# Which tiles of a softmax denominator VectorE sums: nine instead of eight in the second and fourth head pair

## The chip, the cores and the metric

The kernel runs on one core of one Trainium2 chip. The metric is the device time of one launch in microseconds (us). Before the change the median of three runs is 4265.29 us (4264.81 to 4266.23).

## The reference, cut to what matters

Two graph attention layers follow each other, each with a residual and a layer norm, on eight batches of 2048 nodes with 256 features.

```python
# layer 0: eight heads of 32 features
e = leaky_relu(e_src[..., :, None] + e_dst[..., None, :], 0.2)
e = e + (softplus(beta_tilde) * log(prior + 1e-6))[:, None, :, :]     # prior = adj
e = where(adj > 0, e, neg_inf)
h = einsum('bhij,bhjf->bhif', softmax(e, -1), x_proj)
x = layernorm(x + h.transpose(...).reshape(B, N, D) @ W_out.T)
# layer 1: one head
e = where(adj > 0, leaky_relu(einsum('bnd,bmd->bnm', x @ W1, x @ W2), 0.2), -1e12)
x = layernorm(x + relu(softmax(e, -1) @ (x @ W3)))
```

A softmax needs a numerator (the weights times the projected features) and a denominator (the sum of the weights). The change concerns how the denominator of layer 0 is summed, and nothing else.

## The kernel before, in words

**Layer 0, the class `Gat`.** The eight heads are worked in four pairs (`hp` = 0 to 3), and each pair in 16 steps (`jt` = 0 to 15), one for each tile of 128 source nodes j. A step makes one tile `s` of 128 x 2048 float32 for each of the two heads, on VectorE (L391). Its 128 partitions are the nodes j, its 2048 columns the nodes i. The operands are a broadcast row `c` of the head, a per-partition factor `re`, and a tile `mt` of the transposed mask, which a DMA fetches for each step. TensorE then multiplies `s` with the features: `products(self.val, ...)` issues 8 matmuls (the trace shows 16, two for each), which add the numerator up in the PSUM tile `val` over the 16 steps (L424). The denominator is the same product with a weight that does not depend on the feature: `products(self.den, ...)` with `e[:, jt, h]` broadcast to 32 columns, 8 more matmuls into the PSUM tile `den`, also at L424.

**The chain.** A tile j can be taken out of the `den` matmuls and summed elementwise instead. The list `SUMMED[b][hp]`, called `chain` in `step`, holds the tiles of which this is done. In the step of its first tile, ScalarE makes for each head a scaled copy `d = s * e` (L409). For each further tile of the chain, VectorE adds `d = s * e + d` for each head (L404). That update stands one step later in the source: in step `jt` the update is for tile `jt - 1`, behind the two `s` of step `jt`. After step 15 eight matmuls with a weight of ones (L424, `den<-d,ones`) fold the two sums `d` into `den`. A tile in the chain so saves 8 `den` matmuls and costs two passes of VectorE over 128 x 2048 values. The first tile that is not in the chain starts the accumulation in `den`.

**Which tiles.** The first pair has no chain, in any batch. Batch b = 0 has none at all, b = 1 has six tiles in the other three pairs, and b = 2 to 7 have the eight even tiles (0, 2, ... 14) in each of them.

**Layer 1, the class `Dot`.** It takes 128 rows of nodes at a time, 16 row steps for a batch. A row step issues on TensorE four groups of four transposes (`pt`, L590) of the exponentials `p`, between them the scores `e` (L564) of the next row, and then the products with `h3` (`acc`, L607). ScalarE evicts the scores (L566) and the transposes (L592), VectorE applies the mask and finds the row's extreme in one pass over 128 x 2048 values (L569), and ScalarE takes the exponential (L572), which the next row step's transposes wait for.

**How the two are woven.** While batch b - 1 goes through `Dot`, batch b goes through `Gat` (the loop at the end of the kernel). The first pair's steps run beside the output projection and layer norm of layer 0 and the transposes of `turn`. Then `dot.scores(0)` makes the scores of the first row. The first row step takes steps 0 and 1 of the second pair before its transposes and steps 2 and 3 behind its `acc`. Twelve further row steps take 4, 4, 4 (second pair), 3, 3, 3, 3, 4 (third pair) and 3, 3, 3, 3 (fourth pair, whose last 4 are in the thirteenth). Each such group of 3 or 4 steps stands behind the `acc` of its row, so on TensorE all of a group's `val` and `den` matmuls come in one block.

**What sets the order.** TensorE's instructions stand in source order (`tc.manual_schedule`), and from the end of batch 0's layer 0 SyncE's DMA issues too. VectorE's and ScalarE's are placed by the framework when the kernel is built: of what it takes to be ready, it prefers what stands earlier in the source. The trace shows that it moves instructions past each other: of a group's last two `s`, one often stands behind an update of the chain that comes later in the source. [...]

**Buffers.** `s` tiles come from a ring of eight slots, which also holds layer 1's `p` and, for part of a batch, half of `ht`. A slot comes free when its `val` matmuls, its `den` matmuls and, for a chain tile, its update are done. `d` has two slots.

Of the kernel before, what the change touches and what calls it, by code (L numbers as in the profile page):

```python
# [27 lines left out]
def kernel(  # L28
# [27 lines left out]
    B, N, D = x.shape  # L56
    H, _, DH = w_proj.shape
    NT = N // P
# [5 lines left out]
    NP = H // HP  # L64
# [1 line left out]


    SUMMED = [[()] * NP, [()] + [(0, 3, 6, 8, 11, 14)] * (NP - 1)]
    SUMMED += [[()] + [tuple(range(0, NT, 2))] * (NP - 1)] * (B - 2)

    const = ctx.enter_context(tc.tile_pool(name="const", bufs=1))
    dram = ctx.enter_context(tc.tile_pool(name="dram", bufs=1, space=DRAM))
# [695 lines left out]
```

## Time and profile before

| what | value |
|---|---|
| median of the runs | 4265.29 us (4264.81 to 4266.23) |
| the profiled execution: its time, its span | 4269.6 us, 4267.8 us |
| granted TensorE clock | 0.995 |
| TensorE `val` (L424) | 8192 matmuls, 980.3 us busy |
| TensorE `den<-s,re` (L424) | 5600 matmuls, 686.2 us busy |
| VectorE `s` (L391) | 1024 instructions, 2358.4 us busy, 2341 ns each |
| VectorE `d` (L404) | 282 instructions, 654.2 us busy, 2342 ns each |
| ScalarE `d` (L409) | 42 instructions, 84.4 us busy, 2011 ns each |

The busy time of a group is the union of its instructions' spans, and times inside the trace count from the span's start. The `den` matmuls are 350 tiles with 16 matmuls each (512 steps of 8 batches, less 162 tiles in chains). The scaled copies at L409 show how regular the kernel is: those of the second pair start at 1098.24, 1591.89, 2085.83, 2579.86, 3073.66 and 3567.41 us in batches b = 2 to 7. So one of these batches, b = 4, is read closely, and counted six times. There the first `val` matmul of the four pairs starts at 1979.0, 2088.7, 2218.6 and 2345.2 us, and that of the next batch at 2472.6 us.

### The profile page before, as it was taken

What the parts mean: (1) busy time and instruction counts of PE and PEld (TensorE: products, weight loads), DVE (VectorE), ACT (ScalarE), POOL (GpSimd) and SP (SyncE); (2) the same over time, 40 slices, a digit from 0 to 9 for tenths busy, and PEclk for the clock granted to TensorE, in tenths of its full rate; (3) what the DMA queues carried; (4) which work ended last, traced back from release to release, by engine and by line L of the source; (5) the groups of instructions that cost most, each with busy time, mean ns of one, the idle gap of its engine ahead of it and who ended that gap; (6) DMA issues with size and microseconds to landing.
All of it is one profiled execution on the core that took longest, in us unless ns stands there. A gap on an engine that the chain in (4) does not pass through costs nothing.

```text
span 4267.8 us, 59104 instructions
## 1 busy us (share of the span) xinstructions
PE 4169.3 (98%) x24928; PEld 2234.3 (52%) x24928; DVE 3617.9 (85%) x2432; ACT 1606.5 (38%) x3007; POOL 10.3 (0%) x14
## 2 busy tenths in 40 slices
PE   7999999999999999999999999999999999999999
PEld 4444355555555555555555555555455555555766
DVE  6888779998899979999799988999799997998222
ACT  6522133332333333332433333333333323343554
POOL 0000000000000000000000000000000000000000
PEclk9999999999999999999999999999999999999999
DMA  7988756656455565556555474555555565553211
GB/s 240 312 281 322 243 205 225 235 203 238 175 203 201 192 212 181 193 191 226 187 203 194 161 250 166 204 194 204 204 186 189 182 233 180 203 187 136 78 48 40
DMA packets 268458, 843.52 MB, mean 198 GB/s; under 512 B 33184, under 2 KB 166304, under 8 KB 194464
## 3 DMA queue, kind: packets, MB, share of 16 engines
q1 hardware_dynamic: 232352, 806.17, 53.7%
q10 hardware_dynamic: 35840, 33.57, 2.3%
q8 instruction: 195, 3.19, 0.3%
q14 instruction: 71, 0.58, 0.0%
HBM read 763.76 MB, written 75.37 MB: 197 GB/s over the span
## 4 chain that ended last, share of the span: by engine, by line
PE 57%; DVE 26%; issue 8%; DMA 4%; ACT 4%; SPq 0%; DVEq 0%; POOL 0%; ACTq 0%; POOLq 0%
DVE s L391 16%; PE acc L607 13%; PE e L564 12%; PE val L424 12%; PE den L424 8%; DVE d L404 5%; PE pt L590 3%; DMA mt<-mt_d 2%; PE h3p L532 2%; PE proj L283 2%; PE h1p L553 2%; DVE p L569 2%; PE y L493 1%; ACT d L409 1%; DMA adj_r<-in_adj_dram 1%
## 5 line engine op out<-in xcount | busy, mean ns | idle before, releaser
L391 DVE SCALAR_TENSOR_TENSOR s<-c,re,mt 128x2048 f32<-128x2048 f32 x1024 | 2358.4, 2341 | 180.9 <-DMA mt<-mt_d 58.0
L424 PE MATMUL val<-s,v 128*32 128x512 f32 x8192 | 980.3, 598 | 24.1 <-DVE s L391 24.1
L564 PE MATMUL e<-x1t,h 128*128 128x512 f32 x2048 | 964.7, 595 | 6.1 <-ACT pts L592 5.1
L607 PE MATMUL acc<-h,pts 128*128 128x256 f32 x4096 | 907.5, 380 | 0.0
L607 PEld LDWEIGHTS acc<-h,pts 128*128 128x128 f32 x4096 | 779.5, 190 | 157.4 <-issue 57.4
L424 PE MATMUL den<-s,re 128*32 128x512 f32 x5600 | 686.2, 594 | 0.0
L404 DVE SCALAR_TENSOR_TENSOR d<-s,re,d 128x2048 f32<-128x2048 f32 x282 | 654.2, 2342 | 0.0
L424 PEld LDWEIGHTS val<-s,v 128*32 128x32 f32 x8192 | 252.6, 110 | 601.5 <-issue 528.5
L569 DVE CUSTOM_DVE_ANT_0 p<-p,pen 128x2048 f32<-128x2048 f32 x128 | 292.6, 2286 | 256.2 <-ACT p L566 256.1
L564 PEld LDWEIGHTS e<-x1t,h 128*128 128x128 f32 x2048 | 351.2, 190 | 271.7 <-issue 249.8
L566 ACT ACTIVATE p<-e 128x512 f32<-128x512 f32 x512 | 306.1, 598 | 392.9 <-PE e L564 387.5
L572 ACT ACTIVATE p<-p,neg 128x2048 f32<-128x2048 f32 x128 | 256.5, 2004 | 496.8 <-DVE neg L569 496.8
L424 PEld LDWEIGHTS den<-s,re 128*32 128x32 f32 x5600 | 190.3, 110 | 419.4 <-issue 419.0
L590 PEld LDWEIGHTS pt<-ident,p 128*128 128x128 f32 x2048 | 245.5, 141 | 301.1 <-issue 235.8
L592 ACT COPY pts<-pt 128x512 f32<-128x512 f32 x512 | 297.5, 586 | 200.3 <-PE pt L590 193.9
L590 PE MATMUL pt<-ident,p 128*128 128x128 f32 x2048 | 310.2, 276 | 15.7 <-ACT p L572 8.3
L230 ACT ACTIVATE f<-mv,eps_ln 128x1 f32<-128x1 f32 x128 | 37.9, 296 | 432.7 <-DVE mv L228 431.7
L612 ACT ACTIVATE z<-acc,rec 128x256 f32<-128x256 f32 x128 | 60.1, 470 | 288.5 <-issue 127.5
L283 PE MATMUL proj<-wp,xt 128*128 128x272 f32 (+1 forms) x512 | 130.6, 400 | 3.6 <-ACT xt L182 1.8
L532 PE MATMUL h3p<-w3s,x1t 128*128 128x256 f32 x512 | 122.7, 383 | 6.4 <-ACT x1t L527 4.7
L493 PE MATMUL y<-wot,ht 128*128 128x256 f32 x512 | 119.0, 385 | 3.5 <-ACT x1t L527 2.1
L285 ACT COPY v<-proj 128x256 f32<-128x256 f32 x128 | 47.2, 374 | 198.0 <-PE proj L283 153.5
(88 smaller groups left out, 1896.4 us busy)
## 6 DMA issues: line engine op xcount, KB each, us to landing
mt<-mt_d SPq DMA_DIRECT2D x496, 1024.0 KB
c<-c_d SPq DMA_DIRECT2D x64, 1024.0 KB
pen<-pen_d SPq DMA_DIRECT2D x112, 512.0 KB
xg<-in_x_dram SPq DMA_DIRECT2D x60, 512.0 KB
adj_t<-in_adj_dram SPq DMA_DIRECT2D x16, 1024.0 KB
mt_d<-mt SPq DMA_DIRECT2D x16, 1024.0 KB
rb<-rec_d SPq DMA_DIRECT2D x128, 128.0 KB
x_d<-ht ACTq DMA_DIRECT2D x64, 256.0 KB
```

The costliest lines, as they stand in the source:

```text
L283: nc.tensor.matmul(t[:, 0:cols], xt[kc][:, ts(it % IG, P)], wp[:, kc, 0:cols], start=(kc == 0), stop=(kc == KC - 1))
L391: nc.vector.scalar_tensor_tensor(sa, self.cs[a], self.re[:, 0, jt, h:h + 1], mt, ALU.max, ALU.mult)
L404: nc.vector.scalar_tensor_tensor(d, sa, e[:, jt - 1, h:h + 1], d, ALU.mult, ALU.add)
L424: nc.tensor.matmul(dst[ts(q, DH), ts(c, BK)], weights[q % 2], s[q % 2][:, ds(q // 2 * HALF + c * BK, BK)], start=start, stop=stop)
L532: nc.tensor.matmul(t[:, ts(i, D)], x1t[:, kc, ts(2 * (j - lag) + i, P)], w3s[:, kc, :], start=(kc == 0), stop=(kc == KC - 1))
L564: nc.tensor.matmul(t, self.h1[:, kc, ts(it % IG, P)], self.x1t[:, kc, ts(c, BK)], start=(kc == 0), stop=(kc == KC - 1))
L566: nc.scalar.activation(p[:, ts(c, BK)], t, AF.Prelu, alpha=ALPHA)
L569: nc.vector.tensor_tensor_reduce(p, p, pen, -1.0, FMAX, ALU.add, ALU.min, neg)
L572: nc.scalar.activation(p, p, AF.Exp, bias=neg, scale=-1.0, accum_out=den)
L590: nc.tensor.transpose(t[:, ts(k, P)], p[:, ts(g * IG + k, P)], ident)
L592: nc.scalar.copy(pt, t)
L607: nc.tensor.matmul(acc, pts[g][:, ts(k, P)], self.h3[:, j, :], start=(j == 0), stop=(j == NT - 1))
```

## The change

For batches b = 2 to 7, the second pair's chain becomes tiles 0, 1, 2, 3, 6, 8, 10, 12, 14: tiles 1 and 3 come in, tile 4 goes out. The third pair's stays as it was. The fourth pair's becomes 0, 2, 4, 5, 7, 9, 11, 12, 14: tiles 5, 7, 9, 11 come in, 6, 8, 10 go out. Both have nine tiles in place of eight. Batches 0 and 1 are as before. No function changes, only the list that `step` reads.

```diff
     SUMMED = [[()] * NP, [()] + [(0, 3, 6, 8, 11, 14)] * (NP - 1)]
-    SUMMED += [[()] + [tuple(range(0, NT, 2))] * (NP - 1)] * (B - 2)
+    SUMMED += [[(), (0, 1, 2, 3, 6, 8, 10, 12, 14), tuple(range(0, NT, 2)), (0, 2, 4, 5, 7, 9, 11, 12, 14)]] * (B - 2)
```

The lines of `step` that read it:

```python
chain = SUMMED[self.b][hp]
if jt - 1 in chain[1:]:
    for d, sa, h in zip(self.sums, self.last, heads):
        nc.vector.scalar_tensor_tensor(d, sa, e[:, jt - 1, h:h + 1], d, ALU.mult, ALU.add)
...
if jt not in chain:
    self.products(self.den, [e[:, jt, h:h + 1].to_broadcast([P, DH]) for h in heads], s,
                  jt == min(set(range(NT)) - set(chain)), not chain and jt == NT - 1)
```

## The prediction

> **What bounds the kernel now.** I read the page's busy shares first, then one batch (b = 4) by head pair, then the engines' timelines where a wait ends.
>
> ```profile
> PE 4169.3 (98%) x24928; PEld 2234.3 (52%) x24928; DVE 3617.9 (85%) x2432; ACT 1606.5 (38%) x3007; POOL 10.3 (0%) x14
> ```
>
> TensorE (PE) is nearly always busy, and VectorE (DVE) has 15% left. Whether that rest lies where the change puts work is seen from the busy times by stretch (columns: stretch, its length, then busy us and instructions of PE, PEld, DVE, ACT, POOL):
>
> ```profile
> 1979.00:2088.70 109.70, 108.02 (x749) 55.21 (x749) 83.88 (x59) 33.20 (x66) 0.00 (x0) 1.00 0.68 235
> 2088.70:2218.60 129.90, 127.44 (x729) 67.76 (x728) 127.88 (x81) 50.37 (x85) 0.00 (x0) 1.00 0.50 179
> 2218.60:2345.20 126.60, 126.31 (x729) 67.30 (x728) 123.43 (x81) 48.15 (x86) 0.00 (x0) 1.00 0.57 201
> 2345.20:2472.60 127.40, 126.51 (x729) 67.10 (x728) 120.72 (x79) 46.54 (x87) 0.00 (x0) 1.00 0.50 179
> ```
>
> VectorE idles 25.8 us in the first pair, 2.0 in the second, 3.2 in the third, 6.7 in the fourth. So the second pair is bound by both engines at once, and the spare time is mostly in the pair that the change leaves alone. The start of the second pair on VectorE:
>
> ```profile
> 2071.01 4.62 DVE L391 SCALAR_TENSOR_TENSOR s<-c,re,mt 128x2048 f32<-128x2048 f32 x2 [1.04 <-PE den L424]
> 2090.72 2.29 DVE L569 CUSTOM_DVE_ANT_0 p<-p,pen 128x2048 f32<-128x2048 f32 x1 [15.10 <-ACT p L566]
> ...
> 2093.21 9.04 DVE L391 SCALAR_TENSOR_TENSOR s<-c,re,mt 128x2048 f32<-128x2048 f32 x4
> 2102.17 4.61 DVE L404 SCALAR_TENSOR_TENSOR d<-s,re,d 128x2048 f32<-128x2048 f32 x2
> 2106.69 2.28 DVE L569 CUSTOM_DVE_ANT_0 p<-p,pen 128x2048 f32<-128x2048 f32 x1
> ```
>
> Behind the `s` of steps 0 and 1 VectorE stands 15.1 us in front of the mask pass of layer 1's first row, which needs the last score eviction. From 2090.7 on it has no gap until 2323.3. On ScalarE and then TensorE at the same place:
>
> ```profile
> 2085.83 1.99 ACT L409 ACTIVATE d<-s,re 128x2048 f32<-128x2048 f32 x1
> 2087.72 0.59 ACT L566 ACTIVATE p<-e 128x512 f32<-128x512 f32 x1
> 2088.20 2.00 ACT L409 ACTIVATE d<-s,re 128x2048 f32<-128x2048 f32 x1
> 2090.09 0.60 ACT L566 ACTIVATE p<-e 128x512 f32<-128x512 f32 x1
> ```
>
> ```profile
> 2092.12 1.90 PE L424 MATMUL den<-s,re 128*32 128x512 f32 x16
> 2095.20 0.66 PE L590 MATMUL pt<-ident,p 128*128 128x128 f32 x4 [1.18 <-ACT p L572]
> ```
>
> The `d` that an update of tile 1 would continue exists only from 2087.8 (head 0) and 2090.2 (head 1), late in the gap. And TensorE, done with the `den` of tile 1, waits for the exponential. At the end of the second pair (VectorE, then TensorE):
>
> ```profile
> 2186.92 9.13 DVE L391 SCALAR_TENSOR_TENSOR s<-c,re,mt 128x2048 f32<-128x2048 f32 x4
> 2195.97 4.60 DVE L404 SCALAR_TENSOR_TENSOR d<-s,re,d 128x2048 f32<-128x2048 f32 x2
> ```
>
> ```profile
> 2200.62 1.92 PE L424 MATMUL den<-d,ones 128*32 128x512 f32 x14 [0.15 <-DVE d L404]
> ```
>
> The last `s` is ready at 2196.05, and its `val` matmuls start at 2196.02 with the first head: no lead is left. The group before ended with 0.3 us of lead (`s` ready 2164.76, `val` 2165.04), the one before that with 1.9. The end of the fourth pair on VectorE:
>
> ```profile
> 2422.16 9.14 DVE L391 SCALAR_TENSOR_TENSOR s<-c,re,mt 128x2048 f32<-128x2048 f32 x4 [1.98 <-PE den L424]
> ...
> 2442.47 4.61 DVE L404 SCALAR_TENSOR_TENSOR d<-s,re,d 128x2048 f32<-128x2048 f32 x2
> 2447.00 4.61 DVE L391 SCALAR_TENSOR_TENSOR s<-c,re,mt 128x2048 f32<-128x2048 f32 x2
> ```
>
> Here the update of tile 14 was placed ahead of step 15's `s`, which end at 2451.6, and TensorE waits for them (1.8 us between two `val` matmuls).
>
> [...] Here two updates from 2102.17 to the next start at 2106.69 are 2.26 us each, start to start, so listed durations overlap by 0.08; I use 2.26. [...] I therefore price `den` by starts: `val` and `den` alternate at 2067.32, 2069.06, 2070.78 and 2072.49, so 1.72 us each, not the 686.2/350 = 1.96 us of the busy sum.
>
> **The change, part by part.** Per batch it adds two tiles to the chains: VectorE gets 4 updates, 4 x 2.26 = 9.0 us, and TensorE loses 2 x 1.72 = 3.4 us of `den`. Over six batches that is 54 us and 20.6 us. No DMA moves: an update issues none, SyncE's and POOL's queues keep their order, and the copy at L409 stays with tile 0. That `den` in the second pair now starts with tile 4 instead of 1 costs nothing: its eviction was done at 2080. No update carries a wait that is new in kind: it needs an `s` and the `d` before it.
>
> *Second pair, TensorE.* Removing tile 1's `den` (2092.12 to 2093.8) lengthens the wait for the exponential, which still ends at 2095.2: worth nothing. Exchanging tile 3 for tile 4 brings the next row forward by 1.72 us and takes it back in the next group: nothing at tile 7. So TensorE gains 0.
>
> *Second pair, VectorE.* Tile 3's update replaces tile 4's; both stand before step 7's `s`. Tile 1's is 4.52 us more. It is written behind step 2's `s`, and can go forward into the 15.1 us gap only behind its `d`. The framework placed the copies between score evictions, so when step 1's `s` was done it counted the mask pass, which comes first in the source, as ready or nearly. I take it that the update stands behind the mask pass, where nothing idles: +4.52 us for every later `s`. The leads of 1.9, 0.3 and 0.0 turn into TensorE waits that sum to 4.5 us at step 15. The mask pass of the second row may come 4.5 us later too; its exponential then ends near 2115.5, and the transposes, due at 2114.4 without tile 3's `den`, would start before their old 2116.2: no loss. Net **+4.5 us**. Bounds: +1.8 (both updates ahead of the mask pass, 2090.2 + 2.26 against 2090.72), +4.5.
>
> *Third pair.* Both engines come 4.5 us later, so leads stay: 0.
>
> *Fourth pair.* Up to step 11 the updates only change places (leads there 7.8 to 11 us, more than one update). In the last group there are three updates of tiles, 11, 12 and 14, for two before. The extra 4.52 us meets 0.69 + 1.98 = 2.7 us of idle before step 12's `s`. The 1.98 is a wait for a ring slot until tile 9's `den` ended; tile 9 is in the chain now, so the slot is free anyway, and some 0.7 us for the row's residual add stays. I take 2.0 us as absorbed: +2.5 us for step 14's `s`. Step 15's slot comes free 1.72 us sooner and VectorE comes 2.5 later, so step 15's `s` is probably no longer passed by tile 14's update: its `s` ends 2451.6 + 2.5 - 4.5 = 2449.6, and tile 14's update at 2454.1, where the `den<-d,ones` matmuls, due about 2455.1 before, can start. Net **-1.0 us**. If the update stays ahead, step 15's `s` is late by 2.5 us: +2.5. The best is the `den` saved, -1.7.
>
> *Sum.* 6 x (4.5 - 1.0) = +21 us. The profiled execution took 4269.6 us (span 4267.8 and 1.8 around it), 4.3 above the median of the runs, or 0.1%; I put the 21 us on the median: **4286 us**.
>
> **Rivals.**
> *B, both pairs bound by VectorE:* tile 14's update stays ahead. 6 x (4.5 + 2.5) = +42, 4307 us. For it: that is the order now. Against: the shift that I worked out for step 15.
> *C, the update of tile 1 uses the end of the gap:* +1.8 (both heads in it) or +2.26 (one head), with -1.0: 6 x 0.8 to 6 x 1.26, so 4270 to 4273 us; 4291 if the fourth pair goes as in B. For it: updates do pass waiting instructions elsewhere, as at 2442.47.
> *D, faster:* the two copies at L409 move ahead on ScalarE. Their `s` are done at 2065.3 and 2070.0, and ScalarE idles 4.7 us before 2072.7. If the second copy ends by 2086.2, both updates fit in front of 2090.7 for nothing, and the last eviction no longer waits behind a copy: it could run at 2088.8 instead of 2090.09, so the row's exponential and all behind it come 1.3 us sooner. 6 x (-1.3 - 1.0) = -14, 4251 us. Against: what feeds the copies isn't changed by the edit.
> That the edit doesn't do what it says I exclude: `step` reads the list directly.
>
> **How the numbers follow.** Forecast 0.40; B 0.25; C 0.20 (0.07 of it at 4291); D 0.12; worse than 4312 us 0.03. What a measurement of this kernel can tell from no change is about 0.2%, or 8.5 us. Faster: D and a little, 0.13. Same: C at 4270 to 4273, 0.13. Slower: 0.74. The range leaves out D and the worst: 4262 to 4312 us, the lower end being C with the best fourth pair (6 x (1.8 - 1.7), 4266) less 4 us.
>
> **What would show it.** L404 should count 282 + 24 = 306 and `den<-s,re` 5600 - 192 = 5408. Step by step: tile 1's update behind the mask pass at the second pair's start and a wait for the exponential of about 2.9 us instead of 1.18; TensorE's waits for `s` in the second pair summing to some 4.5 us; that pair 134.5 us long instead of 129.9, the third 126.6, the fourth 126.4. I am wrong if the second pair is no longer than before, which would mean updates in the gap, or if the fourth grows, which would mean tile 14's update still ahead of step 15.

## The result and the profile after

The changed kernel takes 4300.3 us (median of 4 runs, 4295.29 to 4304.79), the kernel before 4265.76 us (4 runs, 4264.81 to 4266.41). The ratio is 1.0078, with a 95% interval from 1.0066 to 1.0090: slower by 0.8%, 34.5 us. The forecast was 4286 us.

The busy shares after:

```profile
PE 4166.4 (97%) x24736; PEld 2224.8 (52%) x24736; DVE 3668.9 (85%) x2456; ACT 1606.8 (37%) x3007; POOL 10.7 (0%) x14
```

VectorE's busy time grew by 51 us (24 more updates) and TensorE's shrank by 3 (192 matmuls fewer): L404 counts 306 instructions and `den<-s,re` 5408, as the prediction named them. As a share of the longer span VectorE is where it was and TensorE one point lower. The shares tell nothing of why. The busy times of one batch (b = 4) by head pair do, with the columns as before:

```profile
1987.10:2096.80 109.70, 108.02 (x745) 55.19 (x745) 83.88 (x59) 33.19 (x66) 0.00 (x0) 1.00 0.68 235
2096.80:2231.70 134.90, 127.74 (x713) 66.61 (x712) 132.77 (x83) 50.49 (x85) 0.00 (x0) 1.00 0.49 173
2231.70:2358.90 127.20, 126.44 (x729) 67.32 (x728) 122.70 (x81) 47.76 (x86) 0.00 (x0) 1.00 0.58 198
2358.90:2486.80 127.90, 125.43 (x717) 66.61 (x720) 125.02 (x81) 46.82 (x87) 0.00 (x0) 1.00 0.50 180
```

The second pair went from 129.9 to 134.9 us, with VectorE busy for all but 2.1 us of it, as before. The third grew by 0.6, the fourth by 0.5, though 16 of its matmuls are gone. The start of the second pair, on VectorE:

```profile
2079.54 4.61 DVE L391 SCALAR_TENSOR_TENSOR s<-c,re,mt 128x2048 f32<-128x2048 f32 x2 [0.39 <-DMA mt<-mt_d]
2098.86 2.29 DVE L569 CUSTOM_DVE_ANT_0 p<-p,pen 128x2048 f32<-128x2048 f32 x1 [14.70 <-ACT p L566]
...
2101.34 4.52 DVE L391 SCALAR_TENSOR_TENSOR s<-c,re,mt 128x2048 f32<-128x2048 f32 x2
2105.77 4.61 DVE L404 SCALAR_TENSOR_TENSOR d<-s,re,d 128x2048 f32<-128x2048 f32 x2
2110.30 4.61 DVE L391 SCALAR_TENSOR_TENSOR s<-c,re,mt 128x2048 f32<-128x2048 f32 x2
```

The pair of updates at 2105.77 is tile 1's. It stands behind the mask pass and step 2's `s`; the long gap is as empty as before, and step 3's `s` is pushed back by it. TensorE in the same place, and at the ends of the groups of steps 4 to 7, 8 to 11 and 12 to 15:

```profile
2103.34 0.66 PE L590 MATMUL pt<-ident,p 128*128 128x128 f32 x4 [2.90 <-ACT p L572]
...
2149.59 1.49 PE L424 MATMUL val<-s,v 128*32 128x512 f32 x11 [1.22 <-DVE s L391]
...
2177.47 1.49 PE L424 MATMUL val<-s,v 128*32 128x512 f32 x11 [0.73 <-DVE s L391]
...
2208.76 1.49 PE L424 MATMUL val<-s,v 128*32 128x512 f32 x11 [0.65 <-DVE s L391]
...
2213.28 1.92 PE L424 MATMUL den<-d,ones 128*32 128x512 f32 x14 [0.89 <-DVE d L404]
```

The wait for the exponential is 2.90 us instead of 1.18: it grew by just the 1.72 us of tile 1's `den`. Then each group ends in a wait for an `s` or a `d`, where before there was 0.15 us in all. In these lines the waits for an `s` or a `d` sum to 3.5 us, less than the 4.5 us that the prediction named as a sign; how late the pair's last block is in the end is worked out further below.

Over batches 2 to 7 the pairs' lengths, from the first `val` matmul of a pair to that of the next, sum as follows in the profiled executions (us). For the last pair of batch 7 the length goes to the end of its last `val` matmul. Tables below use the same sums.

| kernel | first pair | second | third | fourth |
|---|---|---|---|---|
| before | 664.8 | 779.9 | 759.5 | 745.7 |
| after | 660.7 | 809.9 | 763.2 | 746.4 |

The difference is 30.3 us (-4.1, +30.0, +3.7, +0.7), and the two profiled executions, 4269.6 and 4300.06 us, are 30.5 apart. The first pair's -4.1 us lies almost wholly in batch 2 (115.8 against 111.6 us) and is not the change's doing: executions with the old first pair show 660 as well as 665. In those with 665, the kernel before among them, the granted clock of TensorE is 0.50 for 6.8 us near the start of that pair (there from 1003.0 us on); in the changed kernel's it isn't.

### The profile page after: what moved, and what is told of

The parts are those of the page before. It is cut to its first block, busy times and chain, and to the rows that moved or that the text cites. A ratio compares the mean times of both kernels' runs of the same rounds, so it can differ in the third digit from the quotient of the medians.

```text
span 4298.3 us, 58706 instructions
## 1 busy us (share of the span) xinstructions
PE 4166.4 (97%) x24736; PEld 2224.8 (52%) x24736; DVE 3668.9 (85%) x2456; ACT 1606.8 (37%) x3007; POOL 10.7 (0%) x14
## 4 chain that ended last, share of the span: by engine, by line
PE 49%; DVE 32%; issue 10%; DMA 5%; ACT 3%; SPq 0%; DVEq 0%; ACTq 0%; POOL 0%; POOLq 0%
DVE s L391 19%; PE acc L607 11%; PE e L564 10%; PE val L424 9%; DVE d L404 8%; PE den L424 8%; PE pt L590 3%; DMA mt<-mt_d 3%; DVE p L569 2%; PE h3p L532 2%; PE proj L283 2%; PE h1p L553 2%; PE y L493 1%; ACT d L409 1%; DMA c<-c_d 1%
## 5 line engine op out<-in xcount | busy, mean ns | idle before, releaser
L424 PE MATMUL val<-s,v 128*32 128x512 f32 x8192 | 1001.2, 599 | 37.1 <-DVE s L391 37.0
L564 PE MATMUL e<-x1t,h 128*128 128x512 f32 x2048 | 968.9, 597 | 13.0 <-ACT pts L592 12.5
L404 DVE SCALAR_TENSOR_TENSOR d<-s,re,d 128x2048 f32<-128x2048 f32 x306 | 712.1, 2343 | 0.0
L424 PE MATMUL den<-s,re 128*32 128x512 f32 x5408 | 676.9, 594 | 0.0
L439 ACT COPY ht<-val 64x1024 f32<-64x1024 f32 x64 | 64.5, 1008 | 202.0 <-PE val L424 198.7
```

Of the source, the lines that this page charges most:

```text
L404: nc.vector.scalar_tensor_tensor(d, sa, e[:, jt - 1, h:h + 1], d, ALU.mult, ALU.add)
L424: nc.tensor.matmul(dst[ts(q, DH), ts(c, BK)], weights[q % 2], s[q % 2][:, ds(q // 2 * HALF + c * BK, BK)], start=start, stop=stop)
L564: nc.tensor.matmul(t, self.h1[:, kc, ts(it % IG, P)], self.x1t[:, kc, ts(c, BK)], start=(kc == 0), stop=(kc == KC - 1))
```

## The experiments

The theory after the result: tile 1's update in the second pair is the whole loss, because VectorE has no gap from the first row's mask pass on, and TensorE gains nothing by tile 1. Its rivals: each ninth tile costs alike; or the crowding of tiles 1, 2, 3 costs. Every ratio is to the kernel before, in runs on the same chip.

**Second pair only.**

```diff
+[(), (0, 1, 2, 3, 6, 8, 10, 12, 14), tuple(range(0, NT, 2)), tuple(range(0, NT, 2))]
```

> Second pair as changed, fourth pair with its old eight even tiles. Theory (the ninth tile's update of the second pair lands in a stretch in which VectorE has no gap, and TensorE gains nothing there): 5.0 us for the second pair and 0.6 for the third behind it, six times: +30 to +34 us, nearly the whole loss. Rival (each of the two ninth tiles costs its two VectorE passes wherever it stands): half of the loss, +15 to +19 us.

Measured: 4302.54 us against 4264.27, ratio 1.0094 (1.0080 to 1.0108). The second pair alone makes the whole loss. At 38 us it is above the 30 to 34 expected, and 4 above both pairs together, though the intervals overlap. The table behind the run with tile 1 alone shows where that comes from.

**Fourth pair only.**

```diff
+[(), tuple(range(0, NT, 2)), tuple(range(0, NT, 2)), (0, 2, 4, 5, 7, 9, 11, 12, 14)]
```

> Fourth pair as changed, second pair with its old eight even tiles. Theory: the ninth tile finds VectorE idle there (6.7 us of 127.4) and TensorE saves 1.7 us less what the last group waits, so -1 to +0.5 us a batch: -6 to +3 us. Rival (each ninth tile costs alike): +15 to +19 us.

Measured: 4264.56 us, ratio 1.0002 (0.9993 to 1.0010). With the second pair as it was, the ninth tile is free in the fourth and worth nothing either. That each ninth tile costs alike is refuted.

**Tile 3 for tile 4.**

```diff
+[(), (0, 2, 3, 6, 8, 10, 12, 14), tuple(range(0, NT, 2)), tuple(range(0, NT, 2))]
```

> Second pair with eight tiles, 0, 2, 3, 6, 8, 10, 12, 14: tile 3 in for tile 4, tile 1 not in the chain. Theory (only tile 1 costs): within 3 us of before. Rival (the chain's tiles standing close together early in the pair hold back the tiles s behind them): +10 us or more.

Measured: 4263.08 us, ratio 0.9999 (0.9991 to 1.0007). The exchange costs nothing.

**Tile 1 alone.**

```diff
+[(), (0, 1, 2, 4, 6, 8, 10, 12, 14), tuple(range(0, NT, 2)), tuple(range(0, NT, 2))]
```

> Second pair with nine tiles, 0, 1, 2, 4, 6, 8, 10, 12, 14: tile 1 in, tile 4 stays, tile 3 is not in the chain. Theory: the same loss as with the second pair changed as a whole, +27 to +34 us. Rival (the crowding of tiles 1, 2, 3 is what costs): +15 us or less.

Measured: 4301.55 us, ratio 1.0088 (1.0074 to 1.0102), as with the whole second pair. The crowding is refuted; it is tile 1. The pairs' lengths in these runs:

| kernel | first pair | second | third | fourth |
|---|---|---|---|---|
| second pair only | 660.4 | 810.1 | 763.2 | 751.3 |
| fourth pair only | 662.3 | 779.9 | 761.5 | 744.7 |
| tile 1 alone | 659.7 | 810.5 | 763.2 | 752.0 |

Both runs with tile 1 in the second pair came out above what was expected of them. Their fourth pair, whose chain is the old one, is about 6 us longer than before (745.7), and longer than the changed kernel's (746.4). The expectations had counted the second pair and the third alone.

The next two take the two sides of tile 1 apart.

**Tile 1's matmuls taken away, without the update.**

```diff
-if jt - 1 in chain[1:]:
+if jt - 1 in chain[1:] and not (self.b > 1 and hp == 1 and jt == 2):
```

> Second pair as with tile 1 alone added (0, 1, 2, 4, 6, ... 14), but tile 1's update is left out too, so its share is missing from that pair's denominators: TensorE is rid of 8 matmuls a batch (1.72 us) and VectorE gets nothing for it. Theory (behind tile 1's matmuls TensorE waits for the exponential anyway): no gain, within 3 us of before. Rival (TensorE is the bound, every block of matmuls taken away is worth its length): -10 us.

Measured: 4271.81 us against 4267.02, ratio 1.0011 (1.0004 to 1.0017). Nothing is gained, and 4.8 us are even lost, a little more than the 3 us expected at most. Where the time went, on TensorE:

```profile
2093.42 1.90 PE L424 MATMUL val<-s,v 128*32 128x512 f32 x16
2098.21 0.66 PE L590 MATMUL pt<-ident,p 128*128 128x128 f32 x4 [2.90 <-ACT p L572]
2098.71 3.09 PE L564 MATMUL e<-x1t,h 128*128 128x512 f32 x4
```

The `den` that is gone became wait, 2.90 us. Then four score matmuls take 3.09 us instead of 1.88: the granted clock (the share of TensorE's full clock, third figure from the end) falls.

```profile
2098.00:2100.00 2.00, 1.79 (x7) 1.04 (x8) 2.00 (x2) 0.75 (x3) 0.00 (x0) 0.81 0.46 170
2100.00:2102.00 2.00, 2.00 (x5) 0.86 (x4) 2.00 (x2) 0.11 (x1) 0.00 (x0) 0.50 0.19 25
2102.00:2104.00 2.00, 2.00 (x8) 1.26 (x7) 2.00 (x2) 1.07 (x2) 0.00 (x0) 0.84 0.86 332
```

This happens in four of the six batches, whose second pair is 131.0 us long. In the other two it is 130.0 us, as before: the matmuls are worth nothing without the fall, too.

**Tile 1's matmuls kept, and the update as well.**

```diff
-if jt not in chain:
+if jt not in chain or self.b > 1 and hp == 1 and jt == 1:
```

(The accumulation in `den` then starts with tile 1.)

> As with tile 1 alone added, but its denominator matmuls are kept as well, so that tile counts twice in that pair's denominators: VectorE gets the update and TensorE is rid of nothing. Theory (the loss is VectorE's alone and the matmuls taken away were worth nothing): the same as tile 1 alone, +33 to +40 us. Rival (the matmuls taken away gave 10 us back, the update cost 47): +44 us or more.

Measured: 4306.23 us against 4267.02, ratio 1.0093 (1.0079 to 1.0107), the same as tile 1 alone within the intervals. With the `den` back, the wait in front of the transposes is the old one:

```profile
2108.78 1.90 PE L424 MATMUL den<-s,re 128*32 128x512 f32 x16
2111.86 0.66 PE L590 MATMUL pt<-ident,p 128*128 128x128 f32 x4 [1.18 <-ACT p L572]
```

So the loss is VectorE's update alone, and the matmuls that it replaces were worth nothing. It isn't the clock either, which could have been the cause as it also falls behind the 2.90 us wait of the changed kernel: in this run it falls in no second pair of batches 2 to 7, and each of them is 134.9 us long, as there.

**The update moved into the gap.** A new function makes `s` of steps 0 and 1, the copies of tile 0 and, where tile 1 is in the chain, its update ahead of the first row's scores. TensorE's order is unchanged. Chains as in the run with the second pair only. (Shown is the call of the new function.)

```diff
+if fresh and b > 1:
+    fresh.early()
 dot.scores(0)
```

> Second pair as changed, fourth as before; in batches 2 to 7 the tiles s of steps 0 and 1, the two scaled copies of tile 0 and tile 1's update stand in the source ahead of the first row's scores, so they are placed ahead of its score evictions and its mask pass. Theory (the update costs because it cannot use the 15 us in which VectorE waits for the last score eviction, as its copy is late): the update lies in that gap, and the last eviction no longer waits behind a copy: -1.3 to +0.5 us a batch, so -10 to +3 us. Rival (nine tiles are one too many for the second pair wherever the update stands): +20 us or more.

Measured: 4269.85 us, ratio 1.0006 (0.9998 to 1.0014): 35 us better than the same chains without it (2.8 us above the kernel before, instead of 38.3). ScalarE makes the copies 20 us sooner, and VectorE puts tile 1's update (here L446) where it had waited:

```profile
2062.75 2.00 ACT L444 ACTIVATE d<-s,re 128x2048 f32<-128x2048 f32 x1 [1.41 <-DVE s L435]
...
2066.74 2.00 ACT L444 ACTIVATE d<-s,re 128x2048 f32<-128x2048 f32 x1 [0.54 <-DVE s L435]
```

```profile
2072.56 4.61 DVE L446 SCALAR_TENSOR_TENSOR d<-s,re,d 128x2048 f32<-128x2048 f32 x2
...
2079.78 6.78 DVE L396 SCALAR_TENSOR_TENSOR s<-c,re,mt 128x2048 f32<-128x2048 f32 x3
...
2086.63 2.29 DVE L597 CUSTOM_DVE_ANT_0 p<-p,pen 128x2048 f32<-128x2048 f32 x1
```

That is the mechanism of rival D of the prediction, and the update is free by it. But the gain that D promised behind it didn't come. The run moves the copies and the update together, so it doesn't show which of the two had kept the update out of the gap. A late copy isn't all of it: in the changed kernel head 0's copy ended at 2095.96, 2.9 us before the mask pass, and VectorE, idle for those 2.9 us, still took its update of 2.26 us behind that pass, in the order placed.

**The same with eight tiles.** To see what the early copies do by themselves: chains as before the change, with the same function.

> The old eight tiles everywhere, with the tiles s of steps 0 and 1 of the second pair and the two scaled copies placed early, as in the run with the copies early and nine tiles. Theory (early copies free the last score eviction, 1.2 us a batch, and that is all they do by themselves): -7 us, and the nine tiles bring nothing on top, so the same as that run within 5 us once its longer third pair is left out. Rival (the ninth tile, once its update is free, gives TensorE's 1.72 us): 10 us slower than the run with nine tiles.

Measured: 4267.08 us against 4267.03, ratio 1.0000 (0.9991 to 1.0008). The ninth tile is worth nothing even when it is free, and the 7 us expected of the early copies didn't come. They do shorten the second pair, and the third gives it back:

| kernel | first pair | second | third | fourth |
|---|---|---|---|---|
| before | 664.8 | 779.9 | 759.5 | 745.7 |
| early, nine tiles | 662.5 | 772.8 | 769.0 | 745.4 |
| early, eight tiles | 661.4 | 770.9 | 772.3 | 745.4 |

With eight tiles TensorE no longer waits at the first transposes of the second pair of batch 4 (with nine it waits 1.58 us there). In the third it waits for ScalarE, twice in this batch:

```profile
2223.42 1.98 PE L592 MATMUL e<-x1t,h 128*128 128x512 f32 x4 [1.47 <-ACT pts L620]
...
2273.63 1.98 PE L592 MATMUL e<-x1t,h 128*128 128x512 f32 x4 [1.41 <-ACT h L583]
```

ScalarE, at the second of them, had the row's norm in front of the eviction, and the norm waited 7.4 us for VectorE:

```profile
2271.03 0.30 ACT L230 ACTIVATE f<-mv,eps_ln 128x1 f32<-128x1 f32 x1 [7.41 <-DVE mv L228]
...
2272.99 1.07 ACT L583 COPY h<-h1p 128x512 f32<-128x512 f32 x2 [0.47 <-ACT z L234]
```

What TensorE wins in the second pair it loses in the third, where ScalarE's queue stands behind VectorE.

**A chain in the first pair.** VectorE's spare time lies there.

```diff
+[(10, 12, 14), tuple(range(0, NT, 2)), tuple(range(0, NT, 2)), tuple(range(0, NT, 2))]
```

> Second to fourth pair as before; the first pair gets a chain of its own in batches 2 to 7, tiles 10, 12, 14: two updates for each head (9.0 us of VectorE), and on TensorE three blocks of denominator matmuls less and one block with ones more (3.4 us less). Theory (spare VectorE time is in the first pair, whose tiles s are 8 us or more ahead there, and TensorE sets its length): -3.4 us a batch, -15 to -20 us. Rival (an update costs what VectorE takes for it, wherever it is put): slower, +20 us or more.

Measured: 4254.54 us against 4267.02, ratio 0.9966 (0.9954 to 0.9979), faster than both kernels. The first pair of the batch read here:

```profile
1977.20:2084.10 106.90, 104.47 (x716) 54.13 (x715) 92.58 (x63) 37.17 (x68) 0.00 (x0) 1.00 0.68 240
```

It is 106.9 us long instead of 109.7: 2.8 of the 3.4 us of matmuls saved are gained, and VectorE has 14 us left over there. The 12.5 us are less than the 15 to 20 expected.

**Four tiles in the first pair.**

```diff
+[(10, 12, 13, 14), tuple(range(0, NT, 2)), tuple(range(0, NT, 2)), tuple(range(0, NT, 2))]
```

> A chain of four tiles, 10, 12, 13, 14, in the first pair of batches 2 to 7, the others as before. Theory (TensorE sets the first pair's length, VectorE has the time): 3 blocks less on TensorE, 5.2 us a batch of which the chain of three kept four fifths: -20 to -28 us. Rival (VectorE's lead there is used up by the third update): no better than the chain of three, -13 us or worse.

Measured: 4264.95 us against 4267.03, ratio 0.9997 (0.9988 to 1.0005). My theory failed here. On VectorE, then TensorE:

```profile
2052.99 4.61 DVE L404 SCALAR_TENSOR_TENSOR d<-s,re,d 128x2048 f32<-128x2048 f32 x2
2057.51 4.61 DVE L391 SCALAR_TENSOR_TENSOR s<-c,re,mt 128x2048 f32<-128x2048 f32 x2
2062.04 4.61 DVE L404 SCALAR_TENSOR_TENSOR d<-s,re,d 128x2048 f32<-128x2048 f32 x2
```

```profile
2062.17 1.49 PE L424 MATMUL val<-s,v 128*32 128x512 f32 x11 [1.22 <-DVE s L391]
...
2066.70 1.92 PE L424 MATMUL den<-d,ones 128*32 128x512 f32 x14 [0.88 <-DVE d L404]
```

The update that this run adds, tile 13's (at 2052.99), stands ahead of step 15's `s`, which had 8.9 us of lead in the kernel before, and the pair ends in the same two waits that the changed kernel shows in its second pair. I had counted the pair's idle time, and most of what is left stands behind the last `s`, in the long gap.

**Four tiles in the first pair, with the early copies.**

> The chain of four tiles in the first pair together with the early copies in the second, eight tiles in the second to fourth pair. Theory: the two gains use different time and add up, -20 to -35 us. Rival (with a chain in the first pair the gap at the second pair's start is filled and the copies have to wait for the two slots of d): no better than the chain of four alone.

Measured: 4267.02 us, ratio 0.9997 (0.9989 to 1.0005). The 20 to 35 us expected didn't come. There was nothing to add up: neither half gives anything alone.

**The same with nine tiles in the second pair.**

> As the run before it, with nine tiles in the second pair (0, 1, 2, 3, 6, ... 14), tile 1's update placed early. Theory: tile 1's update now competes with the first pair's chain for the gap, and TensorE gains nothing by it: 0 to 15 us slower than with eight. Rival (the gap of 15 us holds both): the same within 3 us.

Measured: 4279.44 us, ratio 1.0026 (1.0016 to 1.0036), 12 us slower than with eight tiles, as the theory had it. Two sets of updates do not both fit in front of the second pair: with eight tiles VectorE is idle for only 0.9 us ahead of the mask pass; with nine it has no idle time there, and TensorE then waits 2.61 us for the exponential. The second pairs sum to 783.1 us, against 770.8 with eight tiles.

## Why the prediction was right, and where its sizes were off

**Direction and place: right.** Slower, with the loss in the second pair, by tile 1's update behind the mask pass. Tile 1 alone loses as much as the whole change.

**"So TensorE gains 0": right.** The wait for the exponential went from 1.18 to 2.90 us, as forecast. Taking the matmuls away without an update gained nothing, and keeping them beside the update lost nothing more.

**"+4.5 us" for the second pair: 5.0 measured** (30.0 / 6). From the mask pass to the end of the last `s` VectorE takes 2208.70 - 2098.86 = 109.84 us, before 2196.05 - 2090.72 = 105.33: 4.51 more, the two updates and nothing else. The last block of `den` stands 116.48 us behind the pair's start instead of 111.95, 4.53 more. The rest comes behind it: 0.52 us for a score eviction in front of a later transpose, in both engines' new positions.

**"Third pair: 0": 0.6 measured** (3.7 / 6). I had both engines come 4.5 us later and keep their leads. TensorE came 5.0 us later, and VectorE, which needs TensorE to free a slot, waits for it where it had not:

```profile
2233.70 2.35 DVE L391 SCALAR_TENSOR_TENSOR s<-c,re,mt 128x2048 f32<-128x2048 f32 x1 [0.81 <-PE val L424]
```

As this pair, too, ends without a lead (under 0.1 us at its last `s`, before and after), such a wait goes into the time. TensorE meets the delay first at 2317.07, where it waits 0.46 us for an eviction (`pts`) that stands behind the row's norm, as in the fourth pair below.

**"-1.0 us" for the fourth pair: +0.1 measured** (0.7 / 6). It is made of two parts that nearly cancel, and the run with the second pair only tells them apart. Its fourth pair has the old eight tiles and sums to 751.3 us: +0.9 a batch over the kernel before. With the nine tiles added it is 746.4: -0.8, near the forecast. Each of batches 2 to 6 shows the step: 128.3 to 129.0 us with eight tiles, 127.5 to 127.9 with nine. (Beside the old second pair the nine tiles are worth 0.2 a batch by the same sums, 744.7 against 745.7.)

The +0.9 is a term that the prediction put at nothing: it let the second pair's delay arrive in the later pairs as a mere shift. But VectorE's placed order is another one there. At the start of the fourth pair, before and then after:

```profile
2348.82 0.43 DVE L226 BATCH_NORM_STATS2 st<-z 128x6 f32<-128x256 f32 x1
2349.17 2.33 DVE L391 SCALAR_TENSOR_TENSOR s<-c,re,mt 128x2048 f32<-128x2048 f32 x1
2351.42 0.17 DVE L228 BATCH_NORM_AGGREGATE mv<-st 128x2 f32<-128x6 f32 x1
```

```profile
2362.92 2.34 DVE L391 SCALAR_TENSOR_TENSOR s<-c,re,mt 128x2048 f32<-128x2048 f32 x1
2365.18 0.42 DVE L226 BATCH_NORM_STATS2 st<-z 128x6 f32<-128x256 f32 x1
2365.52 2.33 DVE L391 SCALAR_TENSOR_TENSOR s<-c,re,mt 128x2048 f32<-128x2048 f32 x1
2367.77 0.17 DVE L228 BATCH_NORM_AGGREGATE mv<-st 128x2 f32<-128x6 f32 x1
```

One more `s` stands ahead of the statistics of the row's norm. ScalarE waits longer for them (5.21 us before), and behind the norm stands the eviction that TensorE needs. ScalarE, then TensorE, after:

```profile
2367.98 0.29 ACT L230 ACTIVATE f<-mv,eps_ln 128x1 f32<-128x1 f32 x1 [7.35 <-DVE mv L228]
...
2369.37 0.56 ACT L592 COPY pts<-pt 128x512 f32<-128x512 f32 x1
```

```profile
2369.99 1.98 PE L564 MATMUL e<-x1t,h 128*128 128x512 f32 x4 [1.25 <-ACT pts L592]
```

The kernel before has no such wait there. The run with the second pair only has it, with the same order on VectorE, and no change of the fourth pair:

```profile
2368.61 1.98 PE L564 MATMUL e<-x1t,h 128*128 128x512 f32 x4 [1.06 <-ACT pts L592]
```

In the -0.8, the prediction let step 15's `s` pass both halves of tile 14's update. It passes one. On VectorE, then TensorE:

```profile
2458.87 2.34 DVE L404 SCALAR_TENSOR_TENSOR d<-s,re,d 128x2048 f32<-128x2048 f32 x1
2461.13 4.60 DVE L391 SCALAR_TENSOR_TENSOR s<-c,re,mt 128x2048 f32<-128x2048 f32 x2
2465.66 2.34 DVE L404 SCALAR_TENSOR_TENSOR d<-s,re,d 128x2048 f32<-128x2048 f32 x1
```

```profile
2465.79 1.49 PE L424 MATMUL val<-s,v 128*32 128x512 f32 x11 [1.22 <-DVE s L391]
```

The last `s` ends 106.8 us behind the pair's start (2465.74 - 2358.92), in the run with the second pair only 107.7: 0.9 sooner, where 2.0 was forecast. Against the kernel before (106.4) it is later. The prediction had named a longer fourth pair as a sign of being wrong, and by this sign it was wrong on that pair.

**The sum.** Forecast +4.5, 0, -1.0 a batch, 21 us over six; measured +5.0, +0.6, +0.1, 34 us, near the 34.5 of the medians. Of the 13 us missing, 3 are the second pair, 4 the third, and some 7 the fourth, nearly 6 of them carried into it by the second pair's change. All three terms were too low, so nothing cancelled; the range was wide enough to hold them.

**Rivals.** B (tile 14's update stays ahead in the fourth pair) holds by half. C and D need the update in the gap, and it wasn't there. D's mechanism was shown to work when the source is arranged for it, but its gain was wrong: the 1.3 us in front of the mask pass do shorten the second pair, and are lost again in the third.

## What to carry to other kernels

Where two engines are both nearly full, work moved from one to the other must be weighed at the place where it lands: read the lead of the producer over the consumer at the end of each group, and where it is near zero, every added microsecond is lost, while work taken away in front of a wait is worth nothing. Idle time of the receiving engine counts only if the moved work is ready there: the 15 us gap was useless until the update's input was made earlier and the update itself stood ahead of the mask pass in the source. And a gain in a stretch that another engine paces is to be followed into the next stretches before it is believed. So is a loss: the order that the framework places can change where the source didn't, as in the fourth pair here.

## What the runs showed of the hardware that was not expected

TensorE's granted clock was 0.50 behind single waits of 2.90 us, though TensorE is busy 97% of the time in the changed kernel. In the profiled execution of the kernel without tile 1's matmuls and update, four of the six batches have a stretch of about 3.4 us at 0.50 behind that wait, and its second pairs sum to 783.9 us instead of 779.9, 4.0 of the 4.8 us that the kernel lost. In the changed kernel, with the same wait of 2.90 us, three of six batches show such a stretch, each 3.41 us long and beginning between 0.3 us before the end of the wait and 1.0 us behind it; behind the old wait of 1.18 us no batch of the kernel before does. The waits and stretches in the changed kernel's second pairs:

| batch | 2 | 3 | 4 | 5 | 6 | 7 |
|---|---|---|---|---|---|---|
| start of the wait of 2.90 us, us | 1100.73 | 1600.88 | 2100.44 | 2600.08 | 3099.68 | 3599.18 |
| clock 0.50 from, us | none | 1603.87 | none | 2603.97 | 3102.32 | none |
| length of the second pair, us | 134.93 | 135.09 | 134.92 | 135.09 | 134.93 | 134.93 |

The wait is equally long in all six, so its length does not tell the three batches apart; what does is not shown here. What a fall costs depends on the stretch: 1.0 us in the kernel without tile 1's matmuls and update (131.0 us for a second pair against 130.0), at most 0.2 us in the changed kernel (135.09 against 134.92), whose second pair VectorE fills.
